# Marks of the GINE columns made in the choice of tokens, and layer 0's edge bias added to the weights' rows first

## The chip, the core and the metric

The kernel runs on one core of a Trainium2 chip, as one program launch. The metric is the device time in microseconds. It has five engines with instruction streams of their own: TensorE (PE in the profile, PEld for its weight loads), VectorE (DVE), ScalarE (ACT), GpSimd (POOL) and SyncE (SP, which only issues transfers here). Each runs its instructions in order, and they wait for each other by semaphores.

## The reference, cut to what matters

The whole is four blocks on 10000 nodes of 512 numbers, each added to its input after a layer norm: a relational graph network, a mixture of experts, a GINE network of four layers, and a quantised feed-forward block. The change touches the second and the third.

```python
# mixture of experts, 16 experts, each takes its cap = 625 best tokens of 10000
probs = softmax(x @ gate_w)
scores, tok_idx = lax.top_k(probs.T, 625)           # per expert
toks = x[tok_idx]                                   # gathered
y = (gelu(toks @ w1 + b1) @ w2 + b2) * scores       # per expert
out = zeros.at[tok_idx].add(y) + shared(x)

# GINE, 4 layers, 5000 edges (src, dst, edge_attr), edges sorted by dst
for l in range(4):
    e = edge_attr @ We[l] + be[l]                   # [5000, 1] @ [1, 512] + [512]
    m = relu(x[src] + e)
    agg = segment_sum(m, dst, 10000)
    h = ((1.0 + eps[l]) * x + agg) @ W1[l] + b1[l]
    h = relu(batch_norm(h))
    x = relu(h @ W2[l] + b2[l])
```

All is in float32.

## The kernel before

**Nodes and edges.** The 5000 edges are sorted by destination and cut into 40 tiles of 128 slots. The nodes are renumbered so that the destinations come first, in the order of the edge slots: tile t of the edges adds only into columns 128t to 128t+127 of the node features. A destination whose edges run over a tile's end is handed on from tile to tile: the last column of each tile is kept in `tails`, and `gine_carry` (L1263 to L1283) adds up what is carried within a group of eight tiles.

**Marks.** To sum the edge rows of a tile into its columns, TensorE multiplies the rows x [128 edges, 512] by a matrix `same` [128 edges, 128 columns] of zeros and ones: one where the edge's key equals the column's key. `by_dst["key"]` holds a key for each edge slot, `by_dst["kr"]` one for each column. In layer 0, a tile's `same` is made on the spot: TensorE transposes a broadcast column of `kr` into PSUM (L1243), DVE compares it with the edges' keys (L1244), and SP stores it to `same_d` in HBM (L1245), from where layers 1 to 3 load it (L1240).

**The edge tile** (`gine_edge_tile`, L1228 to L1260), once for each of 40 tiles in each of four layers, in the order of the code: POOL gathers the 128 source rows from `xg_d` into one of four buffers `x` (L614); DVE makes x = We*attr + x (L1234); in layer 0 alone POOL adds the bias row `be` (L1236), since the rows of later layers are stored with the next layer's bias in them already (L1426, `row_tile`); ACT takes the relu (L1237); TensorE multiplies by `same` in eight passes (L1248) into one of two PSUM buffers `ps_x`, which layer 0's transposes (L1243) share; DVE adds the sums to the features (L1252, and L1256 for the last column); ACT copies the tail (L1260).

**The products.** The features stay in SBUF, transposed, as `feat` [128, 4, 10000]. A product with a 512x512 weight goes pair by pair over ten pairs of column blocks (`product`, L1305 to L1385): seven block multiplies of eight TensorE passes each (all L1317), in the order ps_e, then six more into ps_d and ps_b, ACT's evictions (L1325), DVE's sums and differences (L1330 to L1351) and two of POOL's (L1352, L1365). The pairs are taken in the order 5 to 9, then 0 to 4; edges reach only into pairs 0 to 4. `products` lays the edge tiles beside the multiplies, in six steps of a product:

```python
        for i, p in enumerate(order):
            last, g = g, make(p)
            next(g)
            if last:
                next(last, None)
            for step in range(6):
                beside(i, step)
                if step < 5:
                    next(g)
```

In layer 0 the edges of a pair run beside the product of the pair just ahead of it, because the first four products have the loading of the rows beside them (`first_edges` is 4): the pair's own product begins right after the carry of its edges. In layers 1 to 3 the edges of pairs 0 to 4 run beside the products of pairs 5 to 9, five products ahead of where they are needed. A scheduler orders each engine's instructions from this; no order is written out by hand there.

**The choice of tokens** (L1000 to L1140) comes ahead of the experts, and ahead of GINE. Probabilities are transposed (L1060), and a threshold for each expert is searched bit by bit, 30 steps: DVE compares and counts (L1082), TensorE sums the counts over partitions (L1068), DVE takes the next bit (L1094, L1096). Then come ties, ranks by scans (L1112, L1123), a store of the ranks to HBM (L1124), a table loaded from it, and for each expert `look_up` (L1154 to L1173), which yields its token numbers `tok`. The experts follow: POOL gathers `x_tok` (L614), TensorE transposes, and so on; POOL scatters the results.

During the search POOL works on the edges' sources (`place_sources`): 40 scatters of node positions `pos_d` (L593), and then 40 gathers `gp` (L614), turned into the indices `gpos` by L610. They stand on POOL's queue ahead of the experts' gathers.

Of the kernel before, what the change touches and what calls it, by code (L numbers as in the profile page):

```python
# [8 lines left out]
F32 = mybir.dt.float32  # L9
# [3 lines left out]
AF = mybir.ActivationFunctionType  # L13
OP = mybir.AluOpType
AX = mybir.AxisListType
PSUM = bass.MemoryType.PSUM

P = 128
N = 10000
D = 512  # L20
KC = D // P
E = 5000
ET = 40
# [46 lines left out]
def gnn_ffn_kernel(ctx: ExitStack, tc: tile.TileContext, I, out, dram):  # L70
    nc = tc.nc
# [17 lines left out]
    same_d = dram("same_d", [P, ET, P])  # L89
# [5 lines left out]
    ident = lasting.tile([P, P], F32, name="ident")  # L95
# [22 lines left out]
    ones = consts.tile([P, P], F32, name="ones")  # L118
# [22 lines left out]
    def row_broadcast(pool, d, width, name):  # L141

        t = pool.tile([P, width], F32, name=name)
        nc.sync.dma_start(t, bass.AP(tensor=d.tensor, offset=d.offset, ap=[[0, P], [1, width]]))
        return t
# [467 lines left out]
    def gather(dst, src, idx):  # L613
        return nc.gpsimd.indirect_dma_start(  # L614
            out=dst, out_offset=None, in_=src, in_offset=bass.IndirectOffsetOnAxis(ap=idx, axis=0)
        )
# [136 lines left out]
    with ExitStack() as s:  # L753
# [3 lines left out]
        wk = s.enter_context(tc.tile_pool(name="sort", bufs=1))  # L757
        place_wk = s.enter_context(tc.tile_pool(name="place_wk", bufs=1))
        ps = s.enter_context(tc.tile_pool(name="sort_ps", bufs=2, space=PSUM))
        with ExitStack() as n:  # L760
# [8 lines left out]
            for d in (r1_d, a2_d, xf_d, x2_d):  # L769
                clear_spare(zero, d)  # L770
            root = load_square(fix, I["L0_gnn_root1"], "root")
            bias = row_broadcast(fix, I["L0_gnn_bias1"], D, "bias")
# [4 lines left out]
            by_dst = sort_edges(  # L777
                "d", I["dst"], I["src"], I["edge_weight1"].rearrange("e o -> (e o)"), by_dst_d, wk, ps,
                meta_pool,
            )  # L780
# [31 lines left out]
    with ExitStack() as n:  # L812
        wk = n.enter_context(tc.tile_pool(name="q_wk", bufs=1))
        ps = n.enter_context(tc.tile_pool(name="q_ps", bufs=1, space=PSUM))
# [30 lines left out]
    with ExitStack() as s:  # L845
# [14 lines left out]
        with ExitStack() as n:  # L860
# [9 lines left out]
            bias = row_broadcast(fix, I["L0_gnn_bias2"], D, "bias")  # L870
# [109 lines left out]
            for b in range(NB + 1):  # L980
                if b < NB:
                    halves[b] = first_half(b)
                if b:
                    second_half(b - 1, *halves.pop(b - 1))
                    if b % 5 == 0:
                        t0, t1 = 4 * (b - 5), min(4 * b, NT)
# [21 lines left out]
        def by_tile(dst, d):  # L1008

            for i in range(PARTS):  # L1010
                nc.sync.dma_start(
                    dst[i * PER : (i + 1) * PER],
                    d[i * EXPERTS : (i + 1) * EXPERTS, :].rearrange("e (g p) -> g e p", p=P),
                )

        with ExitStack() as n:
            wk = n.enter_context(tc.tile_pool(name="top_wk", bufs=1))
# [38 lines left out]
            for g0 in range(0, PER, 4):  # L1056
                ps = pt.tile([P, 4, P], F32, name="ps_p")
# [5 lines left out]
            nc.sync.dma_start(prob_d, flat)  # L1063
            by_tile(table[:, :, P + 1 :], prob_d)

            def total(c):
                ps = pc.tile([P, 2], F32, name="ps_c")
                nc.tensor.matmul(ps[:, 0:1], lhsT=same_e, rhs=c, start=True, stop=True)  # L1068
                return ps[:, 0:1]
# [21 lines left out]
            for bit in range(top, -1, -1):  # L1091
                have = total(marked(ind, OP.is_ge, thr.bitcast(F32)))
                drop = oh.tile([P, 1], I32, name="drop")
                nc.vector.tensor_scalar(drop, have, float(CAP), float(1 << bit), op0=OP.is_lt, op1=OP.mult)  # L1094
                nxt = oh.tile([P, 1], I32, name="cand")
                nc.vector.scalar_tensor_tensor(  # L1096
                    nxt, drop, (1 << bit) >> 1, thr, op0=OP.bitwise_xor, op1=OP.bitwise_xor
                )
                thr = nxt
# [7 lines left out]
            above_n = marked(sel, OP.is_gt, thr)  # L1107
            need = wk.tile([P, 1], F32, name="need")
            nc.vector.tensor_scalar(need, total(above_n), -1.0, float(CAP), op0=OP.mult, op1=OP.add)
            off = before_run(marked(tie, OP.is_equal, thr))  # L1110
            one_row = ones[:, :1].to_broadcast([P, run])
# [4 lines left out]
                taken, flat_rank, need, tie, op0=OP.is_le, op1=OP.mult, accum_out=taken_n[:, 0:1]  # L1116
# [6 lines left out]
            nc.vector.tensor_tensor_scan(flat_rank, one_row, sel, before_run(all_n), OP.mult, OP.add)  # L1123
            nc.sync.dma_start(rank_d, flat_rank)  # L1124
            by_tile(table[:, :, :P], rank_d)

            bound = wk.tile([P, 2, PER], F32, name="bound")
            nc.vector.tensor_sub(bound[:, 0, :], rank[:, :, 0], sel.rearrange("p (g t) -> p g t", t=P)[:, :, 0])
            nc.vector.tensor_copy(bound[:, 1, :], rank[:, :, P - 1])
            for i in range(2):  # L1130
# [5 lines left out]
                ps = pc.tile([P, EXPERTS], F32, name="ps_c")  # L1136
# [5 lines left out]
        with ExitStack() as n:  # L1142
            tp = n.enter_context(tc.tile_pool(name="ex_tp", bufs=2))
            wk = n.enter_context(tc.tile_pool(name="ex_wk", bufs=6))
# [35 lines left out]
            for e in range(EXPERTS):  # L1180
# [4 lines left out]
                for c, n_ in chunks:  # L1185
                    x = wk.tile([P, D], F32, name="x_tok")
                    gather(x[:n_], xf_d, tok[:n_, e, c : c + 1])
                    ps = pt.tile([P, KC, P], F32, name="ps_t")
# [40 lines left out]
    def gine_edge_tile(l, t, wk, px, we, be, scaled, tail):  # L1229


        x = wk.tile([P, D], F32, name="x", bufs=4)
        gather(x, xg_d, by_dst["gpos"][:, t : t + 1])
        nc.vector.scalar_tensor_tensor(x, we, by_dst["attr"][:, t : t + 1], x, op0=OP.mult, op1=OP.add)  # L1234
        if be is not None:
            nc.gpsimd.tensor_tensor(x, x, be, OP.add)  # L1236
        nc.scalar.activation(x, x, AF.Relu)  # L1237
        same = wk.tile([P, P], F32, name="same", bufs=4)
        if l:
            nc.sync.dma_start(same, same_d[:, t, :])  # L1240
        else:
            ps_k = px.tile([P, P], F32, name="ps_x")
            nc.tensor.transpose(ps_k, by_dst["kr"][:, t : t + 1].to_broadcast([P, P]), ident)  # L1243
            nc.vector.tensor_scalar(same, ps_k, by_dst["key"][:, t : t + 1], None, op0=OP.is_equal)  # L1244
            nc.sync.dma_start(same_d[:, t, :], same)  # L1245
        ps_a = px.tile([P, KC, P], F32, name="ps_x")
        for k in range(KC):
            nc.tensor.matmul(  # L1248
                ps_a[:, k, :], lhsT=x[:, k * P : (k + 1) * P], rhs=same, start=True, stop=True
            )  # L1250
        zt = big[:, :, t * P : (t + 1) * P]
        nc.vector.scalar_tensor_tensor(  # L1252
            zt[:, :, : P - 1], zt[:, :, : P - 1], one_eps[:, l : l + 1], ps_a[:, :, : P - 1],
            op0=OP.mult, op1=OP.add,
        )
        nc.vector.scalar_tensor_tensor(  # L1256
            zt[:, :, P - 1], ps_a[:, :, P - 1], by_dst["carried"][:, 1, t : t + 1], scaled[:, :, t],
            op0=OP.mult, op1=OP.add,
        )
        nc.scalar.copy(tail, ps_a[:, :, P - 1])  # L1260
# [194 lines left out]
    with ExitStack() as s:  # L1455
        banks = s.enter_context(tc.tile_pool(name="banks", bufs=1, space=PSUM))
        px = s.enter_context(tc.tile_pool(name="px", bufs=2, space=PSUM))
# [19 lines left out]
        for l in range(LAYERS):  # L1477
# [3 lines left out]
            with ExitStack() as n:  # L1481
# [23 lines left out]
                def beside(i, step):  # L1505
                    p = i - first_edges
                    if p < 0:
                        for t in shared_out(units[5:], i * 6 + step, first_edges * 6):
                            first_rows(t, ld, small)
                    elif p < EDGE_PAIRS:  # L1510
                        if p == 0 and step == 0:
                            if l == 0:
                                n0.close()
                            begin_edges()
                        for j in shared_out(range(PT), step, 6):
                            gine_edge_tile(
                                l, p * PT + j, at["wk"], px, at["we"], at["be"], at["scaled"],
                                at["tails"][:, p, :, j + 1],
                            )
                        if step == 5:  # L1520
                            gine_carry(p, at["wk"], at["tails"])
# [12 lines left out]
            if l < LAYERS - 1:  # L1534
                A = load_weights(l, 1)
                with ExitStack() as n:
                    rows = n.enter_context(tc.tile_pool(name=f"gr_{l}", bufs=4))
                    be = row_broadcast(rows, I["L1_gnn_be"][l + 1], D, "be")
# [7 lines left out]
    with ExitStack() as n:  # L1546
        wk = n.enter_context(tc.tile_pool(name="gc_wk", bufs=2))
# [3 lines left out]
        pm = n.enter_context(tc.tile_pool(name="gc_pm", bufs=1, space=PSUM))  # L1551
# [269 lines left out]
```

## Time and profile before

| | us |
|---|---|
| median of 3 runs | 4662.56 (4658.36 to 4666.1) |
| profiled execution, its own time | 4666.98 |
| its span | 4665.2 |
| mean granted TensorE clock | 0.931 of full |
| busy: PE, DVE, ACT, POOL | 4046.1, 2820.7, 1679.5, 1569.0 |
| layer 0's edge stage, 2282.4 to 2511.4 | 229.0 |
| the same stage in layers 1, 2, 3 | 164.0, 164.6, 166.8 |
| search of the threshold, starts of the first and the last of its 30 counts (L1068) | 1687.80 and 1762.81 |

The span runs from the first to the last instruction in the trace; the execution's own time is 1.8 us longer. In rows of the timeline the first number is the start, the second the duration, and the bracket holds the idle time of that engine ahead of it and what ended it. In the list of waits the three numbers are the idle time in total, how often, and the longest. In rows of groups they are the busy time with the mean of one in ns, and then the idle time by what ended it. Durations of matmuls include the pipeline's end, so the spacing of starts says more about throughput.

### The profile page before, as it was taken

Reading aid. Unit: us, or ns where it says so; the run is one execution under the profiler, and the core shown is the slowest. Engines: PE = TensorE matmul, PEld = TensorE weight load, DVE = VectorE, ACT = ScalarE, POOL = GpSimd, SP = SyncE. Lnnn points to the kernel's source line nnn. Section 1 sums busy time; section 2 is a strip of 40 time slices with the busy share of each in tenths; the row PEclk is TensorE's granted clock in tenths of the full one; section 3 lists DMA queues with packets and bytes.
Section 4 is the critical chain, followed back from the end, with each engine's and each line's share of the span. In section 5 each row is a group of like instructions: output and inputs, shape, how many; then the busy total and the mean of one; then the engine's idle time right before and its main releaser. Section 6 shows DMA issues by size and latency. Waiting matters only on the chain.

```text
span 4665.2 us, 42798 instructions
## 1 busy us (share of the span) xinstructions
PE 4046.1 (87%) x13624; PEld 2048.0 (44%) x13624; DVE 2820.7 (60%) x5906; ACT 1679.5 (36%) x2992; POOL 1569.0 (34%) x1127
## 2 busy tenths in 40 slices
PE   6799568897999945968887999999999999999997
PEld 3443234443444422434443555545555455544443
DVE  7887865554545465646755546644575455755776
ACT  4334112232333310116423523354233532334775
POOL 3434334441000036865542113311142111422443
PEclk9899789898988866989889999999999999999998
DMA  8677654457555414986411123102231012311332
GB/s 276 228 260 258 216 123 88 86 105 184 192 171 182 146 48 84 162 164 218 153 54 43 73 77 119 42 17 81 85 108 37 27 75 104 90 30 46 110 109 98
DMA packets 293120, 556.20 MB, mean 119 GB/s; under 512 B 41216, under 2 KB 71969, under 8 KB 291871
## 3 DMA queue, kind: packets, MB, share of 16 engines
q1 hardware_dynamic: 219632, 364.67, 23.2%
q0 software_dynamic: 73264, 188.79, 17.8%
q8 instruction: 111, 1.82, 0.2%
q14 instruction: 113, 0.93, 0.1%
HBM read 292.40 MB, written 260.95 MB: 119 GB/s over the span
## 4 chain that ended last, share of the span: by engine, by line
PE 38%; DVE 8%; DMA 4%; ACT 3%; issue 2%; POOL 1%; POOLq 0%; DVEq 0%; ACTq 0%
PE ps_b L1317 15%; PE ps_d L1317 8%; PE ps_o L1593 5%; PE ps_e L1317 4%; PE ps_x L1424 2%; DMA x<-xg_d,gpos 2%; PE ps_x L1248 2%; ACT feat L1413 1%; DMA x_in<-x_d,node_at 1%; DVE stats L1402 1%; DVE x L1234 1%; DVE feat L1252 1%; PE ps_q L1661 1%; DVE feat L1332 1%; DVE t L1340 0%
## 5 line engine op out<-in xcount | busy, mean ns | idle before, releaser
L1317 PE MATMUL ps_b<-feat,w 128*128 128x512 f32 (+1 forms) x1120 | 499.7, 587 | 25.6 <-ACT feat L1413 25.5
L1317 PE MATMUL ps_d<-feat,w_s 128*128 128x512 f32 (+1 forms) x1120 | 503.6, 586 | 4.3 <-issue 3.1
L1325 ACT ACTIVATE feat<-ps_b,cols 128x512 f32<-128x512 f32 (+1 forms) x300 | 203.8, 683 | 568.1 <-PE ps_b L1317 555.4
L1352 POOL TENSOR_TENSOR feat<-feat 128x1024 f32<-128x1024 f32 (+1 forms) x70 | 162.5, 2322 | 623.2 <-DVE feat L1351 598.2
L1365 POOL TENSOR_TENSOR feat<-feat,p 128x1024 f32<-128x1024 f32 (+1 forms) x70 | 176.3, 2519 | 483.0 <-ACT feat L1325 474.2
L637 DVE SCALAR_TENSOR_TENSOR w<-basis,att,w 128x2048 f32<-128x2048 f32 x116 | 315.8, 2731 | 15.6 <-DMA basis<-in_L_gnn_basis 15.6
L742 PE MATMUL ps_o<-root,xT 128*128 128x512 f32 (+1 forms) x632 | 323.6, 625 | 0.0
L1317 PEld LDWEIGHTS ps_b<-feat,w 128*128 128x128 f32 x1120 | 208.4, 191 | 255.5 <-issue 209.4
L703 PE MATMUL ps_o<-w,aT 128*128 x656 | 304.6, 609 | 0.1
L1426 DVE TENSOR_TENSOR x_rows<-ps_x,be 128x512 f32<-128x512 f32 (+1 forms) x237 | 157.4, 685 | 231.0 <-PE ps_x L1424 231.0
L1317 PEld LDWEIGHTS ps_d<-feat,w_s 128*128 128x128 f32 x1120 | 203.3, 192 | 202.2 <-issue 183.0
L918 PE MATMUL ps_n<-root,rT 128*128 128x512 f32 (+1 forms) x632 | 288.6, 613 | 0.0
L1317 PE MATMUL ps_b<-t,w_s 128*128 128x512 f32 (+1 forms) x560 | 259.2, 603 | 21.7 <-ACT feat L1325 21.6
L1317 PE MATMUL ps_e<-feat,w 128*128 128x512 f32 (+1 forms) x560 | 264.9, 614 | 12.9 <-DVE feat L1283 12.9
L614 POOL DMA_INDIRECT x<-xg_d,gpos x160 | 175.0, 1093 | 287.8 <-issue 71.8
L1317 PE MATMUL ps_b<-feat,w_s 128*128 128x512 f32 (+1 forms) x560 | 253.7, 591 | 0.0
L1413 ACT ACTIVATE feat<-feat,bn_sm 128x512 f32<-128x512 f32 (+2 forms) x320 | 236.6, 809 | 3.4 <-DVE bn_sm L1532 3.4
L1234 DVE SCALAR_TENSOR_TENSOR x<-we,srt_d,x 128x512 f32<-128x512 f32 x160 | 139.9, 889 | 156.6 <-DMA x<-xg_d,gpos 149.5
L1402 DVE BATCH_NORM_STATS2 stats<-feat 128x6 f32<-128x512 f32 (+1 forms) x320 | 202.7, 667 | 46.7 <-POOL feat L1365 33.1
L1248 PE MATMUL ps_x<-same,x 128*128 128x128 f32 x1280 | 176.9, 287 | 58.6 <-DVE same L1244 24.1
L1248 PEld LDWEIGHTS ps_x<-same,x 128*128 128x128 f32 x1280 | 167.9, 199 | 126.9 <-issue 42.2
L1237 ACT ACTIVATE x<-x 128x512 f32<-128x512 f32 x160 | 99.3, 628 | 295.2 <-DVE x L1234 179.3
(483 smaller groups left out, 7656.1 us busy)
## 6 DMA issues: line engine op xcount, KB each, us to landing
basis<-in_L_gnn_basis SPq DMA_DIRECT2D x60, 1024.0 KB
xg_d<-x_rows SPq DMA_DIRECT2D x234, 256.0 KB
xg_d<-x_in SPq DMA_DIRECT2D x39, 512.0 KB
x_in<-in_x SPq DMA_DIRECT2D x19, 1024.0 KB
a_d<-x_in SPq DMA_DIRECT2D x19, 1024.0 KB
xn_d<-xn SPq DMA_DIRECT2D x19, 1024.0 KB
r_d<-o_nodes SPq DMA_DIRECT2D x19, 1024.0 KB
r_in<-r_d SPq DMA_DIRECT2D x19, 1024.0 KB
```

What stands on the lines that cost most here:

```text
L637: nc.vector.scalar_tensor_tensor(ws[:, r], tf, c, ws[:, r], op0=OP.mult, op1=OP.add)
L703: nc.tensor.matmul(ps_o, lhsT=aT[:, k, :], rhs=w_all[:, bass.ds(w0 + k * D, D)], start=k == 0, stop=k == KC - 1,)
L742: nc.tensor.matmul(ps_o[:n], lhsT=xT[:, k, a * P : a * P + n], rhs=root[:, k, :], start=k == 0, stop=k == KC - 1,)
L918: nc.tensor.matmul(ps_o[:n_], lhsT=rT[:, k, a * P : a * P + n_], rhs=root[:, k, :], start=k == 0, stop=k == KC - 1,)
L1234: nc.vector.scalar_tensor_tensor(x, we, by_dst["attr"][:, t : t + 1], x, op0=OP.mult, op1=OP.add)
L1248: nc.tensor.matmul(ps_a[:, k, :], lhsT=x[:, k * P : (k + 1) * P], rhs=same, start=True, stop=True)
L1317: nc.tensor.matmul(ps[fo], lhsT=A[a][:, k, fo * P : (fo + 1) * P], rhs=x[:, k, :], start=first and k == 0, stop=k == 1, skip_group_check=True,
L1325: nc.scalar.activation(dst[:, fo, :], ps[fo], func, bias=b, scale=scale)
L1365: nc.gpsimd.tensor_tensor(b22, b22, p5, OP.add)
L1402: nc.vector.bn_stats(stats[:, k, 2 * p + j, :], big[:, k, s0 + j * w : s0 + (j + 1) * w])
L1413: nc.scalar.activation(hb, hb, AF.Relu, bias=sm[:, fo, 3:4], scale=sm[:, fo, 2:3])
L1593: nc.tensor.matmul(ps_o[:n_], lhsT=big[:, kc, t * P : t * P + n_], rhs=W2[kc], start=kc == 0, stop=kc == KC - 1,)
```

## The change

The 40 `same` matrices are made ahead of time, within the choice of tokens, in ten groups of four tiles, and by other engines: TensorE transposes the columns' keys as before, ACT squares the difference from the edge's key and takes relu(1 - d*d), which is one where the keys (whole numbers) are equal and zero elsewhere. A store per group brings them to `same_d`. All four layers now load `same` from there, into one of three buffers instead of four. In layer 0 the bias goes to the row of edge weights first: ACT makes e = We*attr, POOL adds `be` to e, and DVE adds e to the gathered row. `e` has one buffer.

```diff
+            def mark_columns(t0, mk, pm):
+                m = mk.tile([P, 4, P], F32, name="marks")
+                ps = pm.tile([P, 4, P], F32, name="ps_m")
+                for j in range(4):
+                    t = t0 + j
+                    nc.tensor.transpose(ps[:, j, :], by_dst["kr"][:, t : t + 1].to_broadcast([P, P]), ident)
+                for j in range(4):
+                    nc.scalar.activation(
+                        m[:, j, :], ps[:, j, :], AF.Square, bias=minus_key[:, t0 + j : t0 + j + 1], scale=1.0
+                    )
+                nc.scalar.activation(m, m, AF.Relu, bias=ones[:, 0:1], scale=-1.0)
+                nc.sync.dma_start(same_d[:, t0 : t0 + 4, :], m)
...
             nc.sync.dma_start(rank_d, flat_rank)
             by_tile(table[:, :, :P], rank_d)
+            minus_key = wk.tile([P, ET], F32, name="minus_key")
+            nc.gpsimd.tensor_scalar(minus_key, by_dst["key"], -1.0, None, op0=OP.mult)
+            mk = n.enter_context(tc.tile_pool(name="top_mk", bufs=2))
+            pm = n.enter_context(tc.tile_pool(name="top_pm", bufs=2, space=PSUM))
+            for t0 in range(0, ET, 4):
+                mark_columns(t0, mk, pm)
...
         gather(x, xg_d, by_dst["gpos"][:, t : t + 1])
-        nc.vector.scalar_tensor_tensor(x, we, by_dst["attr"][:, t : t + 1], x, op0=OP.mult, op1=OP.add)
-        if be is not None:
-            nc.gpsimd.tensor_tensor(x, x, be, OP.add)
+        attr = by_dst["attr"][:, t : t + 1]
+        if be is None:
+            nc.vector.scalar_tensor_tensor(x, we, attr, x, op0=OP.mult, op1=OP.add)
+        else:
+            e = wk.tile([P, D], F32, name="e", bufs=1)
+            nc.scalar.activation(e, we, AF.Identity, bias=0.0, scale=attr)
+            nc.gpsimd.tensor_tensor(e, e, be, OP.add)
+            nc.vector.tensor_add(x, x, e)
         nc.scalar.activation(x, x, AF.Relu)
-        same = wk.tile([P, P], F32, name="same", bufs=4)
-        if l:
-            nc.sync.dma_start(same, same_d[:, t, :])
-        else:
-            ps_k = px.tile([P, P], F32, name="ps_x")
-            nc.tensor.transpose(ps_k, by_dst["kr"][:, t : t + 1].to_broadcast([P, P]), ident)
-            nc.vector.tensor_scalar(same, ps_k, by_dst["key"][:, t : t + 1], None, op0=OP.is_equal)
-            nc.sync.dma_start(same_d[:, t, :], same)
+        same = wk.tile([P, P], F32, name="same", bufs=3)
+        nc.sync.dma_start(same, same_d[:, t, :])
```

## The prediction

> **What bounds the kernel now.** I read the page's engine shares first, then the windows of the four GINE edge stages (from a layer's first product beside edges to its last), then layer 0's waits and groups, its TensorE timeline, and last the timeline of the token choice. TensorE is busy for 87% of the span, so only places where it stands still can give anything. Layer 0's edge stage is one:
>
> ```profile
> PE 4046.1 (87%) x13624; PEld 2048.0 (44%) x13624; DVE 2820.7 (60%) x5906; ACT 1679.5 (36%) x2992; POOL 1569.0 (34%) x1127
> ...
> 2282.40:2511.40 229.00, 178.81 (x621) 101.14 (x619) 149.62 (x270) 59.89 (x129) 119.42 (x90) 0.87 0.22 60
> 2825.30:2989.30 164.00, 149.81 (x590) 87.10 (x588) 119.58 (x229) 61.21 (x127) 67.73 (x50) 0.99 0.29 82
> ```
>
> The columns are window, length, busy time of PE, PEld, DVE, ACT, POOL, granted clock, DMA. The same five pairs of products take 229 us in layer 0 and 164 us in layer 1. Layer 0 has more work on DVE (30 us) and POOL (52 us), and a lower clock: 0.87 against 0.99. What TensorE and its suppliers wait for there:
>
> ```profile
> ACT x L1237 <- POOL x L1236: 115.7, 39, 6.9
> POOL x L1236 <- DVE x L1234: 43.2, 26, 3.5
> PE ps_x L1248 <- DVE same L1244: 24.1, 16, 2.3
> PE ps_e L1317 <- DVE feat L1283: 12.9, 5, 3.9
> PE ps_x L1248 <- ACT x L1237: 9.4, 4, 4.4
> ```
>
> TensorE waits 24.1 us for the marks, 9.4 us for the rectified rows, 12.9 us for the carry ahead of each product. A pair's boundary looks like this:
>
> ```profile
> 2372.41 6.45 PE L1317 MATMUL ps_e<-feat,w 128*128 128x512 f32 x8 [2.91 <-DVE feat L1283]
> 2378.69 3.60 PE L1317 MATMUL ps_d<-feat,w_s 128*128 128x512 f32 x8
> ...
> 2398.27 1.94 PE L1248 MATMUL ps_x<-same,x 128*128 128x128 f32 x8 [2.02 <-DVE same L1244]
> ...
> 2404.48 1.05 PE L1248 MATMUL ps_x<-same,x 128*128 128x128 f32 x8
> ...
> 2420.60 4.64 PE L1317 MATMUL ps_e<-feat,w 128*128 128x512 f32 x5 [3.02 <-DVE feat L1283]
> ```
>
> One period is 48.2 us here; the four from the ps_e at 2324.57 to that at 2511.38 take 186.8, mean 46.7. Eight matmuls take 3.6 us at full clock and 6.45 after the boundary's wait; an edge tile 1.05, or 1.94 after a wait.
>
> The token choice is the other place. TensorE counts once a search step, DVE compares, POOL scatters positions:
>
> ```profile
> 1716.43 0.16 PE L1068 MATMUL ps_c<-cnt,same_e 128*128 128x1 f16 x1 [2.04 <-DVE ind L1082]
> 1732.36 0.97 POOL L593 DMA_INDIRECT pos_d<-slot,node_at  x1 [0.30 <-issue]
> 1738.62 0.16 PE L1068 MATMUL ps_c<-cnt,same_e 128*128 128x1 f16 x1 [3.34 <-DVE ind L1082]
> 1739.23 0.98 POOL L614 DMA_INDIRECT gp<-pos_d,gidx_d  x1 [5.91 <-issue]
> 1790.40 0.22 DVE L1173 SCALAR_TENSOR_TENSOR tok<-at,ps_l,slot_no 128x1 int32<-128x1 f32 x1
> 1795.58 0.21 POOL L610 CAST gpos<-gp 128x40 int32<-128x40 f32 x1 [2.45 <-DMA gp<-pos_d,gidx_d]
> 1796.73 0.96 POOL L614 DMA_INDIRECT x_tok<-xf_d,tok  x1 [0.94 <-issue]
> 1804.63 0.58 ACT L158 COPY xT<-ps_t 128x512 f32<-128x512 f32 x1 [120.54 <-PE ps_t L1190]
> ```
>
> The first tokens are known at 1790.62, but POOL is free to fetch them only at 1795.79: 5.2 us of slack. ACT idles 120 us here.
>
> **The change, part by part.**
>
> *Marks in the choice.* 40 transposes (0.27 us each in layer 0, an estimate of 0.5 at the choice's clock, 0.50), 40 squares of 128x128 from PSUM (nearest row: ACT's copy of 81x128 from PSUM, 0.26), 10 rectifications of 128x512 (0.63) and 10 stores of 256 KB. ACT's 17 us lie in its 120 us of idle; without that cover they would cost 17. But the order of the compiled instructions puts the third group's first transpose between search counts 13 and 14 on TensorE, and with two PSUM buffers it needs the squares of the first group, which need the negated keys, which stand on POOL behind all 40 scatters. The last is issued at 1732.36+0.97=1733.33; with 0.3 of issue and 0.21 (the CAST of the same shape) the keys are there at 1733.85, four squares later it is 1734.9, and count 14 comes at about 1735.4 instead of 1716.43. All of DVE's search is queued behind it. Not all 19 us are lost: before, the steps from 1718.63 to 1738.62 took 5 us each instead of 2.20 while the scatters ended, for a reason that the trace does not show. If that belongs to the time of the scatters, count 15 falls at 1738.9 where before count 19 fell (1738.62): 4 steps of 2.20, 9 us behind. If it belongs to the position in the program, it is paid again, 11 us more: 20. I take 9, as no engine has a new reason to be slow later. Less the slack of 5.2, the first gather is 4 us late (20: 15 late; 5 or less: none). The expert stage after it is bound by POOL (80 gathers of 1.27 and 80 scatters of 1.88 in about 257 us), so this delay goes on to the end. The nine mark stores ahead of the rank's store on SP wait for ACT, which I put some 3 us ahead of that store at 1775.66; the tenth shares DMA with the table's loads: 0 to 1 us. The negation on POOL lies in the 5.91 us of idle ahead of the gp gathers: nothing.
>
> *Layer 0 loses marks.* 40 transposes (starts 0.11 us apart from what follows, 4.4 us of TensorE), 40 comparisons on DVE (13.6 us) and the 24.1 us of waits on them. 40 stores of 64 KB become 40 loads on SP, issued when a buffer of three comes free; layers 1 to 3 load the same way, without a wait of TensorE on them in my reading. Fewer buffers there (4 to 3): a load has the time of two tiles, over 8 us; I cost it at nothing, and at a load latency of 3 us a tile if the tiles come in bursts. The PSUM pair px no longer alternates between transposes and sums, so a tile's sum may start while the one ahead is read: included below.
>
> *Bias ahead of the gathered rows.* ACT gains 40 of 0.63 us (25 us), DVE's scalar_tensor_tensor becomes a plain sum, POOL keeps its 40, on e. With one e buffer and ACT's order relu(t), e(t+1), the chain of a tile is e 0.63, POOL 1.27, sum 0.66, relu 0.63: 3.2 us, 3.5 with four hand-overs. Eight tiles are 28 us a pair; POOL's two own operations (2.35 each) and ACT's evictions (14 of 0.69) lie in between, and at worst all of them count: 42.3. Gathers wait for their buffer (four) as before, but POOL no longer has to see the gathered rows, which takes 1.27 us out of gather-to-relu.
>
> A rule speaks against the new sum. First the rows, layer 0 and then layer 1:
>
> ```profile
> L1234 DVE SCALAR_TENSOR_TENSOR x<-we,srt_d,x 128x512 f32<-128x512 f32 x40 | 43.6, 1104 | 35.9 <-DMA x<-xg_d,gpos 29.2 <-ACT p L1325 6.7
> L1234 DVE SCALAR_TENSOR_TENSOR x<-we,srt_d,x 128x512 f32<-128x512 f32 x40 | 31.3, 798 | 40.7 <-DMA x<-xg_d,gpos 40.4
> ```
>
> Where POOL also adds, it takes 1.10 us, else 0.80. The Trainium skill, "SBUF — State Buffer", section "Who interferes with whom", says that a VectorE instruction with two SBUF inputs and a GpSimd one that reads SBUF lock each other out for a whole instruction. By the rule alone the new sum, again with two SBUF inputs, is priced at 1.10: 0.3 a tile, 12 us in all. But with one e buffer POOL's next add cannot run during the sum that still reads e, so only POOL's own two operations a pair can collide: I take 0.75 and 2 us in all.
>
> *A pair, summed.* TensorE's work at full clock is 7x3.45 + 8x0.89 = 31.3 (spacing of starts). The boundary's wait and slow ps_e stay: 3.0+2.9=5.9. Waits on relu, tails and the slow tiles after them: 1.9+0.7 a pair as now (9.4/5, and 3.4/5 for tails), plus 2.5 of new ones, an estimate: one tile a pair has its sum on DVE behind the product's subtraction L1351 (1.22 us), another its e on POOL behind L1352 (2.35), and of these some 1 and 1.5 us are uncovered: 42.3. Chain and TensorE meet at the same 42.3, so I take 42.7: 4.0 below 46.7, four times 16. The first pair (2282.8 to 2324.6) has no late tile ahead of it: 0.
>
> **Sum.** -16 (layer 0) + 4 (choice) = -12: the profiled execution's 4666.98 (span 4665.2) becomes 4655; against the median of the runs, 4662.56, it is 4650.5. Layer 0 is bounded by -3 (relu takes over nearly every wait) and -55 (the 33 us of a pair in layer 1); the choice by 0 and +15.
>
> **Rivals.**
> 1. *The search pays its slow steps twice.* Then the choice costs +15 and the sum is -1: 4661.5. For it: the reason of these steps is unknown, and DVE shows "issue" in them. Against: they end with the scatters. Chance 0.15.
> 2. *The serial chain takes the place of the removed waits, and the kernel is slower.* With one e buffer a tile's e waits on ACT behind the relu of the tile before, which waits for its gather (3.4 us landing). Each gather that comes late stops e, POOL, sum and relu of all later tiles, where now DVE, POOL and ACT hold three tiles at once. Twice a pair for 3.4 us makes 42.3+6.8=49, 2.4 above now: +10 for four pairs, +2 for the first, +4 from the choice: 4678. It decides from a period of 45.7, where layer 0's gain no longer covers the 4 us. For it: 29.2 us of DVE's waits are on gathers. Against: four x buffers give a gather some 16 us. Chance 0.22.
> 3. *TensorE becomes the bound as in layer 1.* Pairs of 36 us: -43+4, 4624. For it: the clock rises when the waits go. Against: the carry's wait stays, and the e chain alone is 28 to 33. Chance 0.10.
> 4. *The change does little*: relu waits fill the marks' place, -3+4: 4663.5. Chance 0.08.
>
> **The numbers.** The forecast has 0.45 (own range 4642 to 4658). 0.2% is 9.3 us, about what a measurement of this kernel can tell from no change; 4653.2 is its lower edge. Faster: 0.37 of the forecast's 0.45 and rival 3, 0.47. Within: 0.08, rival 1, rival 4 and a little of 2: 0.34. Slower: 0.19. The range, 4628 to 4674, leaves out a part of rivals 2 and 3.
>
> **What would show it.** Right: ps_e periods near 42.7; no wait on marks in layer 0; count 14 near 1735 with TensorE waiting for ACT's square; x_tok's first gather at 1800 to 1801. Wrong: count 15 to 19 again 5 us apart (rival 1); relu waiting on DVE's sum, that on POOL's e, for more than 30 us of a window that is no shorter than 225 (rival 2); window below 185 and clock above 0.95 (rival 3); TensorE waiting on DMA for marks in any layer.

## The result, and the profile after

On the chip of the first comparison the kernel took 4629.68 us (median of 4, 4627.49 to 4632.49) against 4662.22: ratio 0.9943, interval 0.9929 to 0.9957, 32.5 us less. On two other chips the same program gained far less: 0.9989 (0.9974 to 1.0004) and 0.9985 (0.9975 to 0.9995), 6.3 and 5.0 us by the medians. Both facts need an explanation, and a cut by stages gives most of it. Cut at the first transposes of the probabilities, the first gather of tokens, the first ps_e of GINE, and then those of pairs 9, 0 and 4, all in us and each from one profiled execution (the second row of before and "second chip" are of one chip; the third chip has no trace of before):

| | choice | experts | loading | pair 9 to pair 0 | four periods | the rest |
|---|---|---|---|---|---|---|
| before | 115.4 | 305.3 | 166.2 | 56.4 | 186.8 | 2153.8 |
| before, another chip | 117.3 | 302.6 | 160.6 | 56.4 | 179.3 | 2148.0 |
| after | 117.4 | 302.8 | 158.0 | 58.2 | 154.6 | 2154.0 |
| after, second chip | 141.5 | 302.2 | 161.6 | 58.2 | 154.4 | 2150.9 |
| after, third chip | 140.5 | 303.2 | 159.5 | 60.5 | 155.2 | 2154.5 |

The four periods fall by 32 us in the first pair of traces (25 against the second trace of before). The choice costs 2 us more on the first chip and, against either trace of before, 23 to 26 on the others. Experts, loading and the rest also differ between two traces of before by 3, 6 and 6 us, so the 8 us that loading seems to gain are not assigned to any edit. For the same reason not all of the 32.5 us on the first chip is shown to be the change's own. (In the changed kernel the first transposes of the probabilities stand 1.8 us behind two groups of marks, which the column does not hold.)

The four periods, from the ps_e of pair 0 to that of pair 4, window rows of before, of its second trace, and of after (columns: window, length, busy time of PE, PEld, DVE, ACT, POOL, granted clock, DMA share, GB/s):

```profile
2324.60:2511.40 186.80, 149.80 (x503) 80.70 (x503) 118.83 (x210) 46.96 (x101) 88.48 (x65) 0.88 0.18 51
2323.60:2502.90 179.30, 142.96 (x503) 76.43 (x503) 116.54 (x210) 46.90 (x101) 90.18 (x65) 0.93 0.19 53
2320.60:2475.20 154.60, 134.96 (x479) 73.33 (x478) 96.67 (x179) 65.60 (x133) 89.02 (x67) 0.95 0.21 61
```

TensorE stands idle for 19.6 us (154.6 less 135.0 busy), where it stood for 37.0 and 36.3 before: some 17 us of the gain are idle time, the same against both traces. The rest, 8 to 15 us, is busy time: the transposes are gone (4.4 us by the prediction's estimate), and the granted clock is 0.95 instead of 0.88 or 0.93. The 7.5 us between the two traces of before are nearly all busy time too (149.8 and 143.0), at these two clocks. What TensorE waits for in the whole edge stage of after (from 2278 to 2475), in the list of waits:

```profile
ACT x L1263 <- DVE x L1262: 64.8, 38, 5.1
DVE x L1262 <- POOL e L1261: 53.0, 20, 6.4
POOL e L1261 <- ACT e L1260: 43.6, 21, 3.9
PE ps_x L1268 <- ACT x L1263: 17.3, 7, 4.2
PE ps_b L1337 <- ACT feat L1345: 10.2, 7, 3.7
PE ps_e L1337 <- DVE feat L1303: 8.7, 3, 3.1
```

No line of the list names `same`. The first three lines are the serial chain of one e buffer. It costs TensorE the 17.3 us in the fourth line, and all of that lies ahead of pair 0's ps_e, where no stock of finished rows exists yet. In the later periods it appears only as the fifth line: ACT evicts late, since e and relu stand ahead of the evictions in its queue. One such period in TensorE's timeline:

```profile
2401.79 3.70 PE L1337 MATMUL ps_e<-feat,w 128*128 128x512 f32 x8 [3.12 <-DVE feat L1303]
2405.33 3.63 PE L1337 MATMUL ps_d<-feat,w_s 128*128 128x512 f32 x8
...
2425.60 1.98 PE L1337 MATMUL ps_b<-t,w_s 128*128 128x512 f32 x4 [1.87 <-ACT feat L1345]
2428.88 1.98 PE L1337 MATMUL ps_b<-t,w_s 128*128 128x512 f32 x4 [1.29 <-ACT feat L1345]
2430.70 1.95 PE L1268 MATMUL ps_x<-same,x 128*128 128x128 f32 x16
2432.48 3.60 PE L1337 MATMUL ps_b<-feat,w 128*128 128x512 f32 x8
```

31.3 us of work, 3.1 at the boundary, 1.9+1.3 for evictions and 1.1 of small gaps are the 38.7. Two tiles run back to back here (x16); before, a transpose stood between one tile and the next on TensorE.

The choice in after, timeline, on the first chip:

```profile
1716.55 0.16 PE L1083 MATMUL ps_c<-cnt,same_e 128*128 128x1 f16 x1 [2.04 <-DVE ind L1097]
1737.61 0.48 PE L1073 MATMUL ps_m<-ident,keyrep 128*128 128x128 f32 x1 [20.90 <-ACT marks L1075]
1737.88 0.21 PE L1083 MATMUL ps_c<-cnt,same_e 128*128 128x1 f16 x1
1740.16 0.16 PE L1083 MATMUL ps_c<-cnt,same_e 128*128 128x1 f16 x1 [1.32 <-DVE ind L1097]
1801.53 0.96 POOL L614 DMA_INDIRECT x_tok<-xf_d,tok  x1 [1.74 <-DVE tok L1194]
```

TensorE stands for 20.9 us at the third group's transpose, with count 14 behind it. From then on the steps take 2.2 to 2.3 us. On the second chip the stall is the same, but the last two steps of the search go wrong:

```profile
1761.78 0.16 PE L1083 MATMUL ps_c<-cnt,same_e 128*128 128x1 f16 x1 [1.07 <-issue]
1772.55 0.16 DVE L1109 TENSOR_SCALAR drop<-ps_c 128x1 int32<-128x1 f32 x1 [10.82 <-remote]
1774.55 0.16 PE L1083 MATMUL ps_c<-cnt,same_e 128*128 128x1 f16 x1 [11.65 <-issue]
1785.46 0.22 POOL L610 CAST gpos<-gp 128x40 int32<-128x40 f32 x1 [2.38 <-DMA gp<-pos_d,gidx_d]
1787.25 0.16 DVE L1109 TENSOR_SCALAR drop<-ps_c 128x1 int32<-128x1 f32 x1 [12.75 <-remote]
```

DVE's next instruction needs only a count that TensorE finished 10.6 and 12.5 us earlier ("remote": the trace names no engine that would have released it). The slow stretch ends some 2 us behind the end of POOL's 40 gathers of positions. In the third chip's trace the same two steps take 13.2 and 14.7 us.

### The profile page after: what moved, and what is told of

Its sections match the earlier page's. It is cut to its first block, busy times and chain, and to the rows that moved or that the text cites. A ratio compares the mean times of both kernels' runs of the same rounds, so it can differ in the third digit from the quotient of the medians.

```text
span 4629.2 us, 42910 instructions
## 1 busy us (share of the span) xinstructions
PE 4040.4 (87%) x13624; PEld 2049.1 (44%) x13624; DVE 2791.9 (60%) x5866; ACT 1722.2 (37%) x3082; POOL 1566.0 (34%) x1128
## 4 chain that ended last, share of the span: by engine, by line
PE 39%; DVE 8%; DMA 3%; ACT 2%; issue 2%; POOL 2%; POOLq 0%; DVEq 0%; ACTq 0%
PE ps_b L1337 15%; PE ps_d L1337 9%; PE ps_o L1613 5%; PE ps_e L1337 4%; PE ps_x L1444 2%; PE ps_x L1268 2%; DMA x<-xg_d,gpos 2%; DVE stats L1422 1%; DMA x_in<-x_d,node_at 1%; PE ps_q L1681 1%; ACT feat L1433 1%; DVE feat L1272 1%; DVE x L1257 1%; DVE feat L1352 1%; DVE t L1360 0%
## 5 line engine op out<-in xcount | busy, mean ns | idle before, releaser
L1371 DVE TENSOR_TENSOR feat<-feat,t 128x1024 f32<-128x1024 f32 (+1 forms) x70 | 83.8, 1198 | 197.5 <-PE ps_b L1337 197.5
L170 DVE BATCH_NORM_STATS2 ln_st<-x_in 128x6 f32<-128x512 f32 (+1 forms) x237 | 159.5, 682 | 59.3 <-DMA x_in<-x_d,node_at 55.6
```

## The experiments

**Marks alone.** The edge tile of before, with `same` loaded in all layers; the choice as in the changed kernel.

```diff
-        attr = by_dst["attr"][:, t : t + 1]
-        if be is None:
-            nc.vector.scalar_tensor_tensor(x, we, attr, x, op0=OP.mult, op1=OP.add)
-        else:
-            e = wk.tile([P, D], F32, name="e", bufs=1)
-            nc.scalar.activation(e, we, AF.Identity, bias=0.0, scale=attr)
-            nc.gpsimd.tensor_tensor(e, e, be, OP.add)
-            nc.vector.tensor_add(x, x, e)
+        nc.vector.scalar_tensor_tensor(x, we, by_dst["attr"][:, t : t + 1], x, op0=OP.mult, op1=OP.add)
+        if be is not None:
+            nc.gpsimd.tensor_tensor(x, x, be, OP.add)
```

> Marks made in the choice, layer 0's edge tile otherwise as before (DVE makes We*attr+x, POOL adds the bias to the gathered rows, then relu). Theory A, the marks: TensorE waited for comparisons that stood on DVE behind sums waiting for gathers, so without them the waits on marks (24.1 us), the transposes (4.4) and the slow tiles after such waits go, and little replaces them; layer 0 periods 40 to 42 against 38.7 in the steady pairs of the changed kernel, total 4640 to 4645. Theory B, the bias: what counted was POOL's add between gather and relu; waits of TensorE on relu then take the marks' place, periods stay at 44 to 47, total 4655 to 4665. Under both, the first count behind the marks is 19 us late, as in the changed kernel, and the first gather of tokens 4.8 us late.

This run and the next three shared a chip, on which the changed kernel itself was not run. Ratio 0.9946 (0.9928 to 0.9963), 26 us below before by the medians. The choice took 118.1, with the stall of 21.0 and no slow steps. Four periods 44.4, 41.1, 41.2 and 40.1, together 166.7. Their window row, and TensorE's waits from pair 9's ps_e to pair 4's:

```profile
2308.50:2475.20 166.70, 143.05 (x478) 76.63 (x478) 99.46 (x179) 45.96 (x101) 92.05 (x66) 0.90 0.20 56
```

```profile
PE ps_b L1332 <- ACT feat L1340: 17.0, 4, 4.7
PE ps_x L1263 <- ACT tails L1275: 7.1, 4, 4.3
PE ps_e L1332 <- DVE feat L1298: 6.2, 4, 1.9
PE ps_x L1263 <- ACT x L1258: 5.2, 2, 4.8
```

So the marks alone take 13 to 20 us off the four periods, and relu did not take their place (5.2 us). In part late evictions did (17.0 us). TensorE's idle time in the four periods is 23.7 us, against 36 to 37 before. Theory A holds for this part.

**Bias alone.** Marks as before; e as in the changed kernel; three buffers for `same` (room in SBUF).

> Bias added to the weights' rows first (one e buffer), marks made in layer 0 as before, three buffers for them; nothing in the choice of tokens. Theory A: waits on marks stay near 24 us and periods at 45 to 47, total 4655 to 4668. Theory B: gathered rows reach relu sooner, the comparisons too (DVE's sum no longer waits as long), periods 40 to 42 and, without the choice's 4.8 us, total 4632 to 4640. If both parts are needed for the 8 us a period, this run and the marks-only run each give less than half of the 32 us.

Ratio 0.9981 (0.997 to 0.9992), 8 us. Pair 9 to pair 0 took 59.8, four periods 177.1, 2 to 10 us below the two traces of before. TensorE's waits over both:

```profile
PE ps_x L1253 <- DVE same L1249: 23.4, 13, 2.2
PE ps_x L1253 <- ACT x L1242: 16.3, 7, 4.2
PE ps_e L1322 <- DVE feat L1288: 6.2, 4, 2.4
```

The waits on marks are whole (24.1 before), and the serial chain's waits come on top. Alone, the bias gives little. Once the marks are gone it gives another 12 us in the four periods (166.7 to 154.6), as theory A has it with a smaller second part. Of these 12 only 4 are idle time (23.7 to 19.6); 8 are TensorE's busy time, with a granted clock of 0.90 in the marks-only trace and 0.95 in the changed kernel. Each of the traces that hold both edits or more has 0.94 to 0.97 there, and before, marks-only and bias-only have 0.88 to 0.93, so the clock goes with the edits; with one trace of each part, how much of it belongs to which is not shown. On this chip the gains of the two parts by the medians, 26 and 8 us, add up to the 34 us of the next run, which holds both.

**The key in the square.** (key - k)^2 is also the square of -k + key, so nothing has to be negated on POOL:

```diff
-            minus_key = wk.tile([P, ET], F32, name="minus_key")
-            nc.gpsimd.tensor_scalar(minus_key, by_dst["key"], -1.0, None, op0=OP.mult)
-    bias=minus_key[:, t0 + j : t0 + j + 1], scale=1.0
+    bias=by_dst["key"][:, t0 + j : t0 + j + 1], scale=-1.0
```

> The changed kernel with the negated keys left out: the square takes scale -1 and the key as its bias, so the marks wait for nothing on POOL. Stall theory: no wait of 20.9 us on TensorE in the search, the first gather of tokens back at about 1797, 4.8 us sooner than in the changed kernel, total about 4625. The slow search steps come back if they belong to the time of the last scatters (four steps of some 5 us before 1739), and are found nowhere if the marks' other work had removed them. Rival: the delay of the first gather is paid back later anyway (first product of GINE was only 2.3 us late), and the total stays at 4629.

Ratio 0.9936 (0.9921 to 0.9951), not to be told from the changed kernel's 0.9943, which was measured on another chip, so the gain of this edit alone is not shown. The stall is gone as expected: no step of the search above 2.4 us, the first gather 1.15 us after the CAST as in before (1.95 in the changed kernel), choice 115.2. That is 2 to 3 us less than in the changed kernel (117.4) and in the two runs beside it with the stall (118.1, 117.7), where 4.8 had been expected. Slow steps did not show at all, in a search that ran at the time of the scatters; they are not in every execution. Experts took 304.1 without the delay and 299.4 to 302.8 with it on the chips without slow steps, which is within what traces of before differ by.

**No bias.**

```diff
-                    at["be"] = row_broadcast(wk, I["L1_gnn_be"][l], D, "be") if l == 0 else None
+                    at["be"] = None
```

> The changed kernel with layer 0's edge bias left out (that part of the sum is missing): DVE makes We*attr+x as in layers 1 to 3, no e, no add on POOL. It bounds what the bias still costs. If the chain of e, add, sum and relu is what keeps layer 0 above the 33 us of a pair in layer 1: waits on relu in the first pair (17.3 us) and on ACT's evictions (3.2 a pair) go, periods 35, first pair 34, total about 4605. If the boundary (each pair's product right behind its carry) and the gathers set it: periods 37 to 38, total 4618 to 4625.

This kernel leaves the bias out and so computes another result. Ratio 0.9893 (0.9875 to 0.9912), 4599.6 us. Pair 9 to pair 0 44.3, four periods 38.9, 37.2, 37.2 and 34.9. So the bias as handled in the changed kernel still costs 14 us ahead of pair 0, and only 6 in the four periods, where the boundary and gathers set the rest: the first theory for the first pair, the rival for the others.

**Before and after once more.**

> The kernel before once more, for its trace. The stage that loads and norms the rows ahead of the edges (first product of GINE to that of pair 9) took 166.2 us in the trace of before and 158.0 in that of after, with the same order of instructions on every engine. If that is how executions differ: 155 to 163 here. If the change shortens it by a way not seen in the order: 166 again. The expert stage, 305.3 us before and 302.8 after, likewise: 305 again if the late start there is paid back, 300 to 303 if executions differ. Layer 0's four periods 186 to 188 in any case.

Loading 160.6, experts 302.6. This trace is of another chip than the first, so it shows that executions or chips differ by this much, without telling the two apart. The four periods took 179.3, not 186 to 188, so the 32 us between the first two traces hold some 7 of such difference, nearly all of it in TensorE's busy time (granted clock 0.88 and 0.93). Three of its search steps took 3.5 to 4.4 us.

> The changed kernel once more, on the chip of the runs beside it. Choice, from the first transposes of the probabilities to the first gather of tokens, 117.4 and layer 0's four periods 154.6 again, as both depend on orders and waits that repeat; the other stages within 5 us. Total against before 0.993 to 0.9945.

> The changed kernel beside the next three on one chip. Its search has been seen to run on at 2.20 us a step behind the stall (choice 117.4), and to lose 23 us more in the last two steps (choice 141.5), with POOL's gathers of positions ending at the same moment. Either of them here; layer 0's four periods 154 to 155 in both.

The four periods repeated to 0.8 us (154.4, 155.2). The choice, of which I had expected 117.4 again on the second chip, took 141.5, and 140.5 on the third; both totals fell short accordingly.

**Two buffers e.**

```diff
-        x = wk.tile([P, D], F32, name="x", bufs=4)
+        x = wk.tile([P, D], F32, name="x", bufs=3)
-            e = wk.tile([P, D], F32, name="e", bufs=1)
+            e = wk.tile([P, D], F32, name="e", bufs=2)
```

> The changed kernel with two buffers e; for the room, the gathered rows have three buffers instead of four. Theory of the serial chain: with one buffer e, ACT, POOL, DVE and ACT work on one tile at a time, 17.3 us of TensorE's waits in the first pair and the waits on ACT's evictions later; with two, the first pair falls from 58.2 to 50 to 54 and the later periods from 38.7 to 37, total 6 to 10 us below the changed kernel. Rival, the gathers: the first pair waits for rows, and three buffers make it worse: 58 to 62, later periods 39 to 41, total 0 to 8 above.

Ratio 1.0007 (0.9995 to 1.0019), 8 us above the changed kernel beside it. Pair 9 to pair 0 fell from 58.2 to 51.1, as the serial chain has it. The four periods did not fall (155.8), with DVE waiting 28.2 us for gathers, and the rest took 2166.0 (15 more than in the run beside it): layers 1 to 3 also have only three buffers for rows. The sum on DVE became dearer as well, 1.01 us on the mean instead of 0.76:

```profile
L1262 DVE TENSOR_TENSOR x<-x,e 128x512 f32<-128x512 f32 x40 | 30.3, 757 | 58.8 <-POOL e L1261 53.0 <-DMA x<-xg_d,gpos 5.8
L1262 DVE TENSOR_TENSOR x<-x,e 128x512 f32<-128x512 f32 x40 | 40.2, 1014 | 41.2 <-DMA x<-xg_d,gpos 28.2 <-POOL e L1261 12.9
```

The first row is of the changed kernel, the second of this run. The chain is real in the first pair. As two buffer counts were changed at once, which of them costs the later time is not separated.

**e on DVE.**

```diff
-            nc.scalar.activation(e, we, AF.Identity, bias=0.0, scale=attr)
-            nc.gpsimd.tensor_tensor(e, e, be, OP.add)
+            nc.vector.scalar_tensor_tensor(e, we, attr, be, op0=OP.mult, op1=OP.add)
```

> The changed kernel with e = We*attr + be made by one instruction of DVE (0.75 each by the row of the like sum) instead of ACT's and POOL's two; all else the same. If the hops between three engines are what costs: first pair 46 to 52, no waits of POOL on ACT, evictions on time, later periods 37 to 37.5 as without the bias, total 10 to 15 below the changed kernel. If DVE becomes the bound, its 26 us of a 38.7 us period growing to 32 and its queue holding back what TensorE waits for (carry, sums): later periods 40 to 42, first pair 55, total 0 to 8 above.

Ratio 0.9955 (0.9938 to 0.9972), against 0.9989 beside it, 17 us. Pair 9 to pair 0 49.9; periods 37.1, 36.6, 38.2 and 36.3, together 148.2, as without any bias. Window row of the four periods, and the group of e:

```profile
2319.30:2467.50 148.20, 133.72 (x474) 73.18 (x473) 114.26 (x208) 46.95 (x102) 50.65 (x36) 0.95 0.22 63
```

```profile
L1260 DVE SCALAR_TENSOR_TENSOR e<-we,srt_d,be 128x512 f32<-128x512 f32 x40 | 31.6, 789 | 2.8 <-DMA be<-in_L_gnn_be 2.1
```

DVE works 114 of 148 us and is not the bound. One instruction of 0.79 us in place of 0.71 on ACT and 1.29 on POOL also removes hand-overs between engines.

**Sources early.** POOL's 80 transfers of positions are let in behind the 15th block of the pass ahead of the choice (20 blocks), no longer behind its end:

```diff
-                        softmax(P, t0, full)
+                        early_prob = softmax(P, t0, full)
+                        if b == 15:
+                            at_prob = early_prob
-            place_sources(by_dst, meta_pool, last_prob)
+            place_sources(by_dst, meta_pool, at_prob)
```

> The changed kernel with POOL's 80 scatters and gathers of positions let in behind the 15th of 20 blocks of the pass ahead of the choice instead of behind its end, where POOL idled 115 us; nothing else. If slow steps of the search belong to POOL's series of indirect transfers: no step over 2.4 us in the search, neither the stall of 21 us (the negated keys come early) nor the last two; choice, from the first transposes to the first gather of tokens, 107 to 110 as the search alone sets it, total 8 us below the changed kernel where that has 117 in the choice, 32 below where it has 141. If slow steps belong to the place in the program: the 23 us remain where the changed kernel beside it shows them. The pass ahead may grow by 0 to 10 us as its transfers share the DMA engines with the positions'.

Ratio 1.0007 (0.9997 to 1.0018), against 0.9985 beside it. The search has no step above 2.4 us and the choice takes 98.1, 42 less than beside it. But the pass ahead grew by 53 us. Windows from 1570 to 1680, in the kernel before (first chip) and then here:

```profile
1570.00:1680.00 110.00, 104.32 (x327) 47.98 (x325) 55.25 (x102) 33.73 (x54) 0.00 (x0) 0.95 0.32 115
```

```profile
1570.00:1680.00 110.00, 68.73 (x172) 30.42 (x171) 29.64 (x50) 16.28 (x25) 74.80 (x77) 0.77 0.28 64
```

TensorE runs 172 matmul records instead of 327, at a lower DMA rate, and the list of waits from 1570 to 1735 names what the search had named:

```profile
DVE x_in L922 <- remote: 47.9, 3, 20.8
```

The slow hand-overs moved with POOL's series, in this trace and in that of all three edits below, both of this chip. So the place in the program alone does not make them, and neither does the search; the series is needed. It is not enough: on the chip of the first four runs it ran beside the search without them. I had expected 0 to 10 us for the pass; that was wrong.

**Both gains.** Key in the square and e on DVE:

> The changed kernel with both single edits that gained: the key as the square's bias (no negated keys, so no stall in the search) and e made by one instruction of DVE. They act in different stages, so they should add: choice 115 with POOL's gathers as its end, first pair 50, four periods 148; 17 us below the changed kernel where that has 117 in the choice, up to 40 where it has 141. If slow steps stay in the search (four of 5 us), POOL's gathers hide them, as they did in the kernel before.

Ratio 0.9924 (0.9898 to 0.995), median 4620.34 against 4643.38 for the changed kernel on the same chip: the fastest version, by 23 us. Pair 9 to pair 0 49.7, four periods 144.4: 21.6 us of the 23. The choice took 138.4, not 115: nine steps of up to 5.6 us during the scatters, and then again two of 10.1 and 14.0 as the gathers end. POOL's gathers did not hide them, so the key in the square did not protect from slow steps in this execution.

**All three.**

> All three edits: key in the square, e on DVE, sources early. Choice 107 to 110, first pair 50, four periods 148: 6 us below the version without early sources, if the pass ahead of the choice does not grow; level with it or above if that grows by 6 or more.

Ratio 0.9972 (0.996 to 0.9984). Choice 98.5, periods 145.6, and the pass 60 us longer than in the version without early sources: the stated case "level or above", with 23 us above.

## Why the prediction was right, and where not

The direction, the main mechanism and, on the first chip, the range (4628 to 4674) hold, the range by 1.7 us at its fast end. The middle (4650.5, 12 us of gain) was off: layer 0 was sized at half to two thirds of the 25 to 32 us measured, and the choice's risk was put too low. That the total fell into the range is in part luck. The same program gains 32.5 us on one chip and 5 to 6 on two others, where layer 0's gain and the loss in the choice nearly cancel, and on the first chip the total is nearer to rival 3's 4624 than to the forecast.

*A pair, summed* is the term that was mis-sized: 42.7 was put, and the four periods measured 42.3, 38.9, 38.7 and 34.8, mean 38.7. Two parts of it failed. The boundary was put at 5.9, a wait of 3.0 and a slow ps_e of 2.9 more than 3.6. Measured are waits of 2.43, 3.12, 3.12 and 0.62 and ps_e of 5.78, 5.17, 3.70 and 5.40, together 3.7 a period. And 1.9+0.7+2.5 us of waits on relu and tails were put into each pair; in the four periods TensorE has none on relu or tails, but 10.2 us in all, 2.6 a period, on evictions. With the 31.3 of work and 1.1 of small gaps this gives the 38.7. The worst case of the chain (42.3) does not pace these later pairs; finished rows are in stock by then, as I read the absence of waits on relu. Where there is no stock, ahead of pair 0, the chain does show: 17.3 us. That pair was put at 0 and came 1.8 us later; without the bias it would have been 14 us shorter. So the chain was seen, and put into the wrong pairs.

*Layer 0 loses marks* held: the list of waits has none on them in any layer, and three buffers of `same` were enough. The marks-only and bias-only runs show that this was the larger part.

*The rule on the shared port.* The new sum was priced at 0.75 from the data dependence and 1.10 by the rule of the Trainium skill ("SBUF — State Buffer", "Who interferes with whom"). It took 0.757 on the mean, and POOL's add 1.29 where before it took 1.44. With one buffer, POOL's next add of e waits for the sum that reads e, so these two do not meet. With two buffers e they can, and there the sum took 1.01 us on the mean, as the rule would have it; the run did not separate this from its other change.

*The stall.* Count 14 was put 52.7 us behind POOL's first scatter (1735.4 with 1682.72) and came 52.9 behind it (1737.88 with 1685.0). Count 15 followed in 2.28 us, not 3.5, and the first gather was late by 2.5 us from the first scatter, not 4. So far the step was right to 1.5 us. Its bound was not: 15 was named as the worst, from the slow steps of the scatters paid again, and on the two other chips the choice grew by 23 to 24 us against the second trace of before. What fell short is the sentence that no engine has a new reason to be slow later: there the last two steps of the search, beside POOL's gathers, were slow. That is rival 1 in its effect, at a higher price.

Why they are slow stays open. In all five traces that show it (both repeats of the changed kernel, two buffers e, e on DVE, both gains) the stretch begins 27 to 29 us behind the first gather of positions, and it is always the last two steps, so time and place coincide. The runs with early sources show that POOL's series is needed. But gathers alone do not make the stretch. The second trace of before, on the second chip, has its first gather at 1745.52 and its last at 1799.45, and TensorE and VectorE hand over to each other in time 30 us behind the first:

```profile
1775.88 0.39 PE L1137 MATMUL ps_c<-same_e,spread 128*80 128x16 f16 x2 [3.66 <-DVE spread L1132]
1776.15 0.32 DVE L1140 COPY ends<-ps_c 80x16 f32<-80x16 f32 x2 [0.17 <-PE ps_c L1137]
```

That kernel makes no marks in the choice, and its search was over by then; which of the two counts, or whether that execution had no stretch at all, is not shown. Nor is the stall the only way into the stretch: the version with both gains has no stall, but lost some 18 us in slow steps during the scatters, and met it too.

This accounts for the two small ratios: by the table, 20 to 23 us gained from pair 9 to pair 4 against the second trace of before, 23 to 24 lost in the choice. That makes the two kernels about even; the 5 to 6 us that remain are within what the other stages of single traces differ by. What decides whether the stretch is slow on a chip is not shown.

*Rival 2* (the chain makes it slower) is out, but its chain is what the first pair pays; *rival 3* (36 us a pair) was nearer than I gave it: the granted clock rose with the waits gone, to 0.95, as it had it, though the whole stage did not fall below its 185 us (197.0 from 2278 to 2475, at a clock of 0.90). e on DVE reaches 37.

## What to carry to other kernels

Taking a small operation out of an in-order queue can be worth several times its own busy time, where that queue also waits for gathers: 13.6 us of comparisons held up TensorE for 24. When work is moved into an idle stretch, look at what its producer stands behind on its own engine, and whether an algebraic turn removes that producer; and ask what the delayed work will then run beside. For a chain over several engines with one buffer, count the stretches that have no stock of finished rows ahead of them: here the first pair paid nearly all of it. And where TensorE's idle time shrinks, compare its busy time and granted clock over the same window too: here they held 8 to 15 of the 25 to 32 us.

## What the runs showed of the hardware that was not expected

While POOL issues a long series of indirect transfers of 128 single numbers each (40 scatters, 40 gathers, one per 1.25 to 1.47 us), other engines can be late at a hand-over by 1 to 3 us, or by some 7 to 20, with nothing in the trace that they would wait for. POOL is not slowed: its gathers come 1.25 us apart in the five traces with the slow stretch, and 1.36 to 1.38 apart in the others with gathers at that place. The DMA share was 0.03 to 0.30 in the windows that hold them. The slow hand-overs stopped with the series, and went with the series to another stage, but on one chip four different kernels showed none of them. The cause stays open, and so does what makes one execution slow and another not.
